# A cross-attention block on one core: where batch sums are kept, how many buffers two weights have, and when 4 MB of loads are issued

## The chip, the cores and the metric

The kernel runs on one core of a Trainium2 chip. A core has five engines that run side by side, each with its own instruction queue in program order: PE (TensorE, matrix products), DVE (VectorE), ACT (ScalarE), POOL (GpSimd) and SP (SyncE, which here only issues transfers). Sixteen DMA engines move data; SP, POOL and ACT hand them transfers through their queues. The metric is device time in microseconds (us), as the median of several executions; shorter is better. One further execution was recorded by the hardware profiler, and all lines shown come from it.

## The reference

One transformer block, all float32, with 4 batches of 512 rows, width 512, 16 heads of 32, and an MLP of inner width 2048. The mask is all ones. Cut to what matters:

```python
x = layer_norm(hidden, ln1_w, ln1_b)
q, k, v = x @ q_w + q_b, enc @ k_w + k_b, enc @ v_w + v_b      # split into 16 heads
attn = softmax(where(mask, q @ k.T / sqrt(32), lowest))
hidden = (attn @ v) @ cproj_w + cproj_b + hidden               # the batch's sum
y = layer_norm(hidden, ln2_w, ln2_b)
y = gelu(y @ fc_w + fc_b) @ proj_w + proj_b
return hidden + y
```

What matters here is `hidden` after the attention: it is read by the second layer norm, and added once more at the very end, after the MLP.

## The kernel before, in words

**Tiling.** A batch of 512 rows is four tiles of 128 rows (t = 0 to 3). The 16 heads are four groups of four (128 columns). The main loop runs over 16 steps w (batch w // 4, head group w % 4), and each step over four query tiles qt; u = 4w + qt counts them all. For each u, `scores` (L228) makes four score matrices on PE, DVE adds the mask and takes the minimum (L240), ACT takes the exponential (L244), and `turn` (L248) transposes the result in 32 x 32 blocks on DVE (L272). Two query tiles make a pair, number 2w + half. `copies` (L300) then sends the pair through 16 transfers of 136 KB (L314) on SP's queue, which put the blocks where the next product wants them: in the single buffer `pT`, or in the spare space of `gt` or `xe`. `attend` (L337) is the product with V; it is due two or four query tiles after its pair.

**What fills PE between.** For each step three projections are made ahead of it: `prep_k`, `prep_q`, `prep_v` (L191, L200, L211), from weights Wk, Wq, Wv that `load_w` (L181) loads for one head group at a time, 256 KB each. Wk has two buffers, Wq and Wv one each: Wq of step w + 1 is loaded by a call in `prep_q(w)` behind the products that read the old one (L206), and Wv likewise (L221). Then there are the output projection `cproj` (L391), the turning of layer-norm results, and the MLP of batches 0 and 1 in pieces: `fc` (L447) and `proj` (L458), 32 pieces a batch, of about 3.5 us of PE each. The MLPs of batches 2 and 3 run at the end (`last_mlps`, L509).

**The order** is written out by hand. `first[w]` and `later[w]` (L759 to L828) are lists of pieces with costs; L830 to L857 spread them over the four query tiles of the step. Every engine does its share in the order in which the calls are made, and a queue that must wait holds up all behind it. `Q[0]` is the queue for loads: POOL's until step 1, then SP's (L834). A transfer on SP also waits for the eighth one before it to have landed.

**The batch's sum.** For batch 0 the rows of x are loaded in step 3 into tiles `hid` (six buffers), get the bias of the output projection from POOL (`add_row`, L369), then `cproj`'s result from DVE (L396); the MLP later adds to the same tiles. For batches 1 and 2 the rows go to tiles `ct` (`load_ct`, L380, which also has POOL add the bias); `cproj` adds to them and stores each tile to a DRAM tensor `xa` (L398). The layer norm works in place in tiles 2 and 3, and on copies of tiles 0 and 1 loaded back from `xa` (`load_yn`, L400). When the MLP needs the sum, `load_hid` (L371) loads all four tiles back from `xa`. Batch 3 is like 1 and 2, with its sum taken to a tile of its own at the end.

**Before step 0** (L732 to L756) SP issues Wk, the encoder rows, Wv, x, Wq, the bias rows and the mask of batch 0. POOL issues Wk of step 1. The eight first MLP weights (2 MB) are POOL's, in step 0 (`load_mlp`, L436); the output projection's weights `wc` (1 MB) are SP's, in step 2; the `hid` rows of batch 0 (1 MB) SP's, in step 3.

Of the kernel before, what the change touches and what calls it, by code (L numbers as in the profile page):

```python
# [44 lines left out]
P = 128  # L45
# [29 lines left out]
def xattn_block(ctx: ExitStack, tc: tile.TileContext, x, encT, mask, q_w, k_w, v_w, c_w, fc_w, p_w, vecs, rows, out):  # L75
# [105 lines left out]
    def load_w(w, queue=None, names=("wk", "wq", "wv")):  # L181

        if w >= NW:
            return
        g = w % NG
        for n, src in (("wk", k_w), ("wq", q_w), ("wv", v_w)):
            if n in names:
                S[n, w] = (two if n == "wk" else one).tile([P, ND, P], F32, tag=n, name=f"{n}_{w}")
                (queue or Q[0]).dma_start(out=S[n, w], in_=src[:, g, :, :])
# [10 lines left out]
    def prep_q(w):  # L200
        b, g = divmod(w, NG)
        qT = kqp.tile([P, L], F32, tag="qT", name=f"qT_{w}")
        acc = acc_tile(f"accq_{w}")
        for d in range(ND):
            nc.tensor.matmul(acc, S["wq", w][:, d, :], xT[:, d, :], start=(d == 0), stop=(d == ND - 1))  # L205
        load_w(w + 1, names=("wq",))  # L206

        nc.scalar.activation(qT, acc, AF.Identity, bias=qb[:, g : g + 1], scale=-scale)  # L208
        S["qT", w] = qT

    def prep_v(w):  # L211
# [9 lines left out]
        load_w(w + 1, names=("wv",))  # L221
# [148 lines left out]

    def load_hid(b, ts_):  # L371

        for t in ts_:
            if ("hid", b, t) not in S:
                S["hid", b, t] = hids.tile([P, D], F32, tag="hid", name=f"hid_{b}_{t}")
            Q[0].dma_start(out=S["hid", b, t], in_=S["xa", b][ts(t, P), :] if b else x[b, ts(t, P), :])
        for t in ts_:
            add_row(S["hid", b, t], 1 if b else 0)

    def load_ct(b, *ts_):  # L380

        for t in ts_:
            if t == 0:
                S["xa", b] = dram.tile([L, D], F32, tag=f"xa{b}", name=f"xa{b}")
            pool, tag = (tiles, "xn") if b == B - 1 or t > 1 else (two, "ct")
            S["ct", b, t] = pool.tile([P, D], F32, tag=tag, name=f"ct_{b}_{t}")
            Q[0].dma_start(out=S["ct", b, t], in_=x[b, ts(t, P), :])
        for t in ts_:
            add_row(S["ct", b, t], 0)

    def cproj(b, t):  # L391
        h = S["ct" if b else "hid", b, t]
        acc = acc_tile(f"accc_{b}_{t}")
        for g in range(NG):
            nc.tensor.matmul(acc, S["oT", b][:, g, ts(t, P)], wc[:, g, :], start=(g == 0), stop=(g == NG - 1))  # L395
        nc.vector.tensor_tensor(h, acc, h, ALU.add)  # L396
        if b:
            (nc.sync if b == B - 1 else nc.gpsimd).dma_start(out=S["xa", b][ts(t, P), :], in_=h)  # L398

    def load_yn(b):  # L400

        S["yn", b] = [S.get(("ct", b, t)) for t in range(NT)]
        for t in range(2):
            S["yn", b][t] = tiles.tile([P, D], F32, tag="xn", name=f"xn2_{b}_{t}")
            Q[0].dma_start(out=S["yn", b][t], in_=S["xa", b][ts(t, P), :])

    def stat2(b, t):
        ln_stat((2, b), t, S["hid", b, t] if b == 0 else S["ct", b, t] if b == B - 1 else S["yn", b][t])

    def norm2(b, t):  # L410
        if b == 0 and t == 0:
            S["yn", b] = [tiles.tile([P, D], F32, tag="xn", name=f"xn2_{b}_{i}") for i in range(NT)]
        if b == B - 1 and t == 0:
            S["yn", b] = [S["ct", b, i] for i in range(NT)]
        ln_norm((2, b), t, S["yn", b][t], S["yn", b][t] if b else S["hid", b, t])

    def proj_bias(b):
        for t in range(NT):
            add_row(S["hid", b, t], 1)
# [274 lines left out]
    def A(w):  # L694
        if w >= NW:
            return []
        return do(lambda: load_w(w + 1, names=("wk",))) + [
# [48 lines left out]
    load_w(1, names=("wk",))  # L746
# [18 lines left out]
    first[0] = do(load_mlp) + do(lambda: load_w(2, names=("wk",))) + [(CHAIN, lambda: prep_v(1)), (CHAIN, lambda: prep_q(1))] + x1 + [load2, k2, q2]  # L765
    first[1] = x2[:1] + [v2, load3, k3] + x2[1:2] + [q3] + x2[2:] + [v3] + x4 + x3
    first[2] = do(lambda: Q[0].dma_start(out=wc, in_=c_w)) + [load4, q4, k4, v4] + A(5)[:2]
# [12 lines left out]
    def ct(b, *ts_):  # L780
        return do(lambda: load_ct(b, *ts_))

    def yn(b):
        return do(lambda: load_yn(b))
# [12 lines left out]
    first[3] = x1 + first[3][:2] + hid_(0, 0, 1, 2, 3) + first[3][2:]  # L797
# [6 lines left out]
    first[5] += t2 + do(lambda: proj_bias(0)) + some(5)  # L804
# [12 lines left out]
    first[10] = [load, k, q] + some(5) + [v] + yn(1)  # L817
# [42 lines left out]
    load_ct(B - 1, *range(NT))  # L860
# [10 lines left out]
    sum_wa(0)  # L871
    run(C(B - 1))
    load_hid(NORMAL, range(NT))
# [46 lines left out]
```

## Time and profile before

| | us |
|---|---|
| median of 3 runs | 839.91 (839.0 to 839.98) |
| the profiled execution's own time | 839.08 |
| its span, first to last instruction | 837.3 |
| PE busy | 813.2 (97% of the span) |
| DVE busy | 555.6 (66%) |
| ACT busy | 342.6 (41%) |
| POOL busy | 103.6 (12%) |
| mean granted PE clock | 0.990 |

The page begins with the busy time of each engine and then cuts the span into 40 slices of 20.9 us; each digit is a busy share in tenths. `PEclk` is the clock that PE was granted, in tenths. Other views are the list of waits (who waited for whom), and timelines of one engine: start, duration, engine, line, operation, tiles written and read, number of instructions, and in brackets the idle time before and what ended it. A product that the code writes as four matmul calls shows as x8; "q" in `SPq` and `POOLq` marks the issuing of a transfer, not its run. The step boundaries in this execution, by the first scores of each: step 1 at 48.8 us, 2 at 78.9, 3 at 101.8, 4 at 137.3, 5 at 178.9, 8 at 291.9, 9 at 337.4, 12 at 448.4.

### The profile page before, as it was taken

How to read it: one execution, taken by the hardware profiler on the slowest of the kernel's cores; microseconds unless marked ns; L12 is line 12 of the kernel's file. 1: busy time of each engine (PE TensorE's matmuls, PEld its weight loads, DVE VectorE, ACT ScalarE, POOL GpSimd, SP SyncE). 2: the span in 40 equal slices, each digit the busy share in tenths (PEclk: the TensorE clock that was granted, in tenths of full speed). 3: DMA queues.
4: the chain of work that ended last, by engine and by line, in shares of the span. 5: the costliest groups of instructions: out<-in, count | busy, mean ns of one | idle time of the engine just before them, and what ended most of it. 6: DMA issues, size and time to landing. Idle time of an engine off the chain costs nothing.

```text
span 837.3 us, 11995 instructions
## 1 busy us (share of the span) xinstructions
PE 813.2 (97%) x4064; PEld 473.7 (57%) x4064; DVE 555.6 (66%) x1259; ACT 342.6 (41%) x740; POOL 103.6 (12%) x122
## 2 busy tenths in 40 slices
PE   9998979799999989999999999999999999999998
PEld 6545544545444544454545445444446888888887
DVE  3597977687666666766787676787425998168511
ACT  2556554336663554346534556464301331023300
POOL 2501003102000020200010410000022003100011
PEclk9999989999999998999999999999999999999999
DMA  5658597665777766677786976885835551032001
GB/s 205 210 151 242 126 255 207 175 153 144 189 177 212 191 185 181 184 196 187 185 221 158 293 185 161 212 194 134 223 122 190 170 184 44 9 92 76 14 13 38
DMA packets 59164, 135.83 MB, mean 162 GB/s; under 512 B 12080, under 2 KB 14256, under 8 KB 58976
## 3 DMA queue, kind: packets, MB, share of 16 engines
q1 hardware_dynamic: 55920, 125.35, 55.2%
q0 software_dynamic: 2656, 8.59, 3.0%
q10 hardware_dynamic: 528, 1.14, 0.6%
q8 instruction: 32, 0.52, 0.3%
q14 instruction: 28, 0.23, 0.1%
HBM read 60.84 MB, written 7.34 MB: 81 GB/s over the span
## 4 chain that ended last, share of the span: by engine, by line
PE 89%; DVE 4%; SPq 3%; DMA 3%; issue 1%; POOL 0%; ACT 0%; DVEq 0%; ACTq 0%; POOLq 0%
PE accp L461 13%; PE accf L451 13%; PE q L555 12%; PE sc L235 7%; PE av L357 7%; PE accc L395 7%; PE accq L205 6%; PE accv L217 5%; PE acck L196 5%; SPq L314 3%; PE tp L137 2%; PE q4p L595 2%; PE q3p L595 2%; PE q5p L595 2%; PE q6p L595 2%; PE q1p L595 2%
## 5 line engine op out<-in xcount | busy, mean ns | idle before, releaser
L244 ACT ACTIVATE s<-s,mn 128x512 f32<-128x512 f32 x256 | 181.6, 710 | 157.2 <-DVE mn L240 156.9
L240 DVE CUSTOM_DVE_ANT_0 s<-sc,mb 128x512 f32<-128x512 f32 x256 | 161.3, 686 | 52.4 <-PE sc L235 52.4
L272 DVE STREAM_TRANSPOSE tb<-s 128x512 f32<-128x512 f32 x240 | 152.6, 683 | 4.2 <-ACT s L244 4.2
L451 PE MATMUL accf<-yT,fcw 128*128 128x512 f32 x256 | 115.3, 600 | 0.4 <-DVE yT L140 0.4
L461 PE MATMUL accp<-pw,gt 128*128 128x512 f32 x256 | 114.3, 598 | 0.0
L451 PEld LDWEIGHTS accf<-yT,fcw 128*128 128x128 f32 x256 | 47.0, 190 | 66.0 <-issue 60.7
L461 PEld LDWEIGHTS accp<-pw,gt 128*128 128x128 f32 x256 | 47.5, 190 | 63.2 <-issue 60.5
L235 PE MATMUL sc<-kT,qT 32*128 32x512 f32 x512 | 73.3, 642 | 1.4 <-ACT qT L208 0.8
L217 PEld LDWEIGHTS accv<-wv,xe 128*128 128x128 f32 x512 | 60.2, 196 | 15.2 <-issue 13.9
L217 PE MATMUL accv<-wv,xe 128*128 128x128 f32 x512 | 62.1, 281 | 5.4 <-DMA wv<-v_w_dram 5.4
L205 PE MATMUL accq<-xe,wq 128*128 128x512 f32 x128 | 60.9, 621 | 4.9 <-DMA wq<-q_w_dram 4.9
L555 PE MATMUL q<-ys,gt 128*128 128x256 f32 x256 | 60.2, 379 | 0.0
L196 PE MATMUL acck<-xe,wk 128*128 128x512 f32 x128 | 58.7, 601 | 0.0
L395 PE MATMUL accc<-wc,oT 128*128 128x512 f32 x128 | 56.8, 596 | 0.0
L357 PE MATMUL av<-pT,v 128*32 128x256 f32 x864 | 53.9, 391 | 0.0
L555 PEld LDWEIGHTS q<-ys,gt 128*128 128x128 f32 x256 | 48.7, 190 | 6.6
L224 POOL TENSOR_TENSOR v<-v,row 128x512 f32<-128x512 f32 x16 | 20.5, 1282 | 238.4 <-ACT v L222 238.4
L465 DVE TENSOR_TENSOR hid<-accp,hid 128x512 f32<-128x512 f32 x32 | 21.9, 684 | 40.2 <-PE accp L461 38.9
L244 ACT ACTIVATION_READ_ACCUMULATOR s<-s,mn 128x1 f32 x256 | 47.7, 186 | 0.0
L205 PEld LDWEIGHTS accq<-xe,wq 128*128 128x128 f32 x128 | 24.5, 198 | 39.1 <-issue 34.9
L555 PE MATMUL q<-yT,gt 128*128 128x256 f32 x192 | 46.4, 379 | 0.0
L244 ACT ACT_TABLE_LOAD x19 | 24.4, 1283 | 47.4 <-DVE mn L240 47.4
(122 smaller groups left out, 870.1 us busy)
## 6 DMA issues: line engine op xcount, KB each, us to landing
pT<-tb SPq DMA_DIRECT2D x400, 136.0 KB, 2.4
pw<-p_w_dram SPq DMA_DIRECT2D x32, 256.0 KB, 3.5
gt<-fc_w_dram SPq DMA_DIRECT2D x32, 256.0 KB, 2.9
gt<-tb SPq DMA_DIRECT2D x48, 136.0 KB, 3.0
fcw<-fc_w_dram SPq DMA_DIRECT2D x24, 256.0 KB, 3.1
xe<-encT_dram SPq DMA_DIRECT2D x16, 256.0 KB, 3.8
pb<-p_w_dram SPq DMA_DIRECT2D x16, 256.0 KB, 4.0
wv<-v_w_dram SPq DMA_DIRECT2D x14, 256.0 KB, 2.9
```

The costliest lines, as they stand in the source:

```text
L196: nc.tensor.matmul(acc, S["wk", w][:, d, :], eT[:, d, :], start=(d == 0), stop=(d == ND - 1))
L205: nc.tensor.matmul(acc, S["wq", w][:, d, :], xT[:, d, :], start=(d == 0), stop=(d == ND - 1))
L217: nc.tensor.matmul(acc[:, ts(t, P)], eT[:, d, ts(t, P)], S["wv", w][:, d, :], start=(d == 0), stop=(d == ND - 1),)
L235: nc.tensor.matmul(sc[:, h, :], qT[r, ts(qt, P)], kT[r, :], start=True, stop=True)
L240: nc.vector.tensor_tensor_reduce(out=s, in0=sc[:, h, :], in1=S["mb", w // NG], scale=1.0, scalar=FMAX, op0=ALU.add, op1=ALU.min, accum_out=mn,
L244: nc.scalar.activation(s, s, AF.Exp, bias=mn, scale=-1.0, accum_out=sums[:, qt, h : h + 1])
L272: nc.vector.transpose(tv[:, q, h], S["ps", w, qt][h])
L357: nc.tensor.matmul(av[ts(h, HD), : 2 * P].rearrange(shape, **kw), v[:, t, ts(h, HD)], p[t][h], start=(t == 0), stop=(t == NT - 1),)
L395: nc.tensor.matmul(acc, S["oT", b][:, g, ts(t, P)], wc[:, g, :], start=(g == 0), stop=(g == NG - 1))
L451: nc.tensor.matmul(acc, S["fcw", b, f][:, d, :], S["yT", b][:, d, :], start=(d == 0), stop=(d == ND - 1))
L461: nc.tensor.matmul(acc, gT[q % 2][:, k, ts(t, P)], S["pw", b, q * FQ + k], start=(k == 0), stop=(k == FQ - 1))
L555: nc.tensor.matmul(o, a[:, k], y[:, k], start=(k == 0), stop=(k == 1))
```

## The change

1. Wq and Wv have two buffers like Wk, and one call at the head of a step's pieces issues the three loads for step w + 1 together. The calls inside `prep_q` and `prep_v` are gone.
2. Before step 0, Wq and Wv of step 1 are issued on POOL's queue beside Wk; and the eight first MLP weights, the rows of x for batch 0's sum, and `wc` (2 + 1 + 1 MB) are issued on SP's queue behind the mask.
3. Tiles 0 and 1 of batches 1 and 2 are loaded into the `hid` buffers and stay there: they aren't stored to `xa`, not loaded back for the layer norm (which now writes to other tiles), and not loaded back for the MLP. Their MLP bias is added by POOL after the layer norm. Tiles 2 and 3 go through `xa` as before.
4. The output projection's bias is no longer added where the rows are loaded but by `c_bias`, called just before `cproj`'s pieces (batch 0: at the end of step 3's).
5. In the MLP's order, step 7 gets six pieces in place of five, so that all later pieces come one place earlier, and in step 11 one piece is moved ahead of the layer norm's turning. The last part of the loop has seven pieces left in place of eight.

In the lists `cb(b)` calls `c_bias(b)`, `h_` calls `load_h`, and `pb_(b)` calls `proj_bias(b)`, which now passes over tiles that don't stay; before, batch 0 alone called it.

```diff
-                S[n, w] = (two if n == "wk" else one).tile([P, ND, P], F32, tag=n, name=f"{n}_{w}")
+                S[n, w] = two.tile([P, ND, P], F32, tag=n, name=f"{n}_{w}")
...
     def prep_q(w):
...
-        load_w(w + 1, names=("wq",))
...
     def prep_v(w):
...
-        load_w(w + 1, names=("wv",))
...
+    def stays(b, t):
+        return b == 0 or b < B - 1 and t < 2
+    def load_h(b, *ts_):
+        if ("xa", b) not in S:
+            S["xa", b] = dram.tile([L, D], F32, tag=f"xa{b}", name=f"xa{b}")
         for t in ts_:
+            pool, tag = (hids, "hid") if stays(b, t) else (tiles, "xn")
+            S["h", b, t] = pool.tile([P, D], F32, tag=tag, name=f"h_{b}_{t}")
+            Q[0].dma_start(out=S["h", b, t], in_=x[b, ts(t, P), :])
+            if stays(b, t):
+                S["hid", b, t] = S["h", b, t]
+    def c_bias(b):
+        for t in range(NT):
+            add_row(S["h", b, t], 0)
     def cproj(b, t):
-        h = S["ct" if b else "hid", b, t]
+        h = S["h", b, t]
...
-        if b:
+        if not stays(b, t):
             (nc.sync if b == B - 1 else nc.gpsimd).dma_start(out=S["xa", b][ts(t, P), :], in_=h)
...
     def norm2(b, t):
+        h = S["h", b, t]
+        y = tiles.tile([P, D], F32, tag="xn", name=f"xn2_{b}_{t}") if stays(b, t) else h
+        S.setdefault(("yn", b), {})[t] = y
+        ln_norm((2, b), t, y, h)
...
     def A(w):
-        return do(lambda: load_w(w + 1, names=("wk",))) + [
+        return do(lambda: load_w(w + 1)) + [
...
     load_mask(0, nc.sync)
-    load_w(1, names=("wk",))
+    load_w(1)
+    Q[0] = nc.sync
+    load_mlp()
+    load_h(0, *range(NT))
+    nc.sync.dma_start(out=wc, in_=c_w)
+    Q[0] = nc.gpsimd
...
-    first[0] = do(load_mlp) + do(lambda: load_w(2, names=("wk",))) + [(CHAIN, lambda: prep_v(1)), (CHAIN, lambda: prep_q(1))] + x1 + [load2, k2, q2]
+    first[0] = do(lambda: load_w(2)) + [(CHAIN, lambda: prep_v(1)), (CHAIN, lambda: prep_q(1))] + x1 + [load2, k2, q2]
-    first[2] = do(lambda: Q[0].dma_start(out=wc, in_=c_w)) + [load4, q4, k4, v4] + A(5)[:2]
+    first[2] = [load4, q4, k4, v4] + A(5)[:2]
-    first[3] = x1 + first[3][:2] + hid_(0, 0, 1, 2, 3) + first[3][2:]
+    first[3] = x1 + first[3] + cb(0)
...
-    first[7] = [load, k, q] + some(5) + [v]
+    first[7] = [load, k, q] + some(6) + [v]
-    first[8] = ct(1, 0, 1) + [load, k] + x2[:1] + [q] + x2[1:2] + some(1) + x2[2:] + [v] + x3 + x4 + ct(1, 2, 3)
-    later[8] = C(1)
+    first[8] = h_(1, 0, 1) + [load, k] + x2[:1] + [q] + x2[1:2] + some(1) + x2[2:] + [v] + x3 + x4 + h_(1, 2, 3)
+    later[8] = cb(1) + C(1)
-    first[10] = [load, k, q] + some(5) + [v] + yn(1)
+    first[10] = [load, k, q] + some(5) + [v]
-    first[11] += norm(1, 2, 3) + some(1) + t2 + [v] + some(1)
+    first[11] += norm(1, 2, 3) + some(2) + t2 + pb_(1) + [v]
-    first[12] = ct(2, 0, 1, 2, 3) + [load, k] + some(3) + hid_(1, 0, 1)
-    later[12] = C(2)
+    first[12] = h_(2, 2, 3, 0, 1) + [load, k] + some(3)
+    later[12] = cb(2) + C(2)
-    first[14] = yn(2) + some(5) + stat(2, 0, 1) + some(2) + stat(2, 2, 3) + rs(2) + some(1)
+    first[14] = some(5) + stat(2, 0, 1) + some(2) + stat(2, 2, 3) + rs(2) + some(1)
-    first[15] = norm(2, 0, 1) + some(4) + norm(2, 2, 3) + some(4) + turns2(2)
+    first[15] = norm(2, 0, 1) + some(4) + norm(2, 2, 3) + some(4) + turns2(2) + pb_(2)
...
-    load_ct(B - 1, *range(NT))
+    load_h(B - 1, *range(NT))
...
+    c_bias(B - 1)
     run(C(B - 1))
-    load_hid(NORMAL, range(NT))
+    load_hid(NORMAL, (2, 3))
```

More of the change, by code (lines that the diff above doesn't have):

```diff
@@ L369, in add_row, with cproj @@
         nc.gpsimd.tensor_tensor(h, h, row[:, i, :], ALU.add)
+    def stays(b, t):
[3 more added lines that the diff above has]
+            S["xa", b] = dram.tile([L, D], F32, tag=f"xa{b}", name=f"xa{b}")
+        for t in ts_:
+            pool, tag = (hids, "hid") if stays(b, t) else (tiles, "xn")
[6 more added lines that the diff above has]
+            add_row(S["h", b, t], 0)
+    def cproj(b, t):
+        h = S["h", b, t]
+        acc = acc_tile(f"accc_{b}_{t}")
+        for g in range(NG):
+            nc.tensor.matmul(acc, S["oT", b][:, g, ts(t, P)], wc[:, g, :], start=(g == 0), stop=(g == NG - 1))
+        nc.vector.tensor_tensor(h, acc, h, ALU.add)
+        if not stays(b, t):
+            (nc.sync if b == B - 1 else nc.gpsimd).dma_start(out=S["xa", b][ts(t, P), :], in_=h)
     def load_hid(b, ts_):
@@ L375, in load_hid @@
                 S["hid", b, t] = hids.tile([P, D], F32, tag="hid", name=f"hid_{b}_{t}")
-            Q[0].dma_start(out=S["hid", b, t], in_=S["xa", b][ts(t, P), :] if b else x[b, ts(t, P), :])
+            Q[0].dma_start(out=S["hid", b, t], in_=S["xa", b][ts(t, P), :])
         for t in ts_:
[L378 to L389, printed above, removed]
@@ L391, in cproj @@
-    def cproj(b, t):
-        h = S["ct" if b else "hid", b, t]
[L393 to L396, printed above, removed]
-        if b:
[L398 to L405, printed above, removed]
+            add_row(S["hid", b, t], 1)
@@ L407, in stat2 @@
     def stat2(b, t):
-        ln_stat((2, b), t, S["hid", b, t] if b == 0 else S["ct", b, t] if b == B - 1 else S["yn", b][t])
+        ln_stat((2, b), t, S["h", b, t])
     def norm2(b, t):
[L411 to L415, printed above, removed]
+        h = S["h", b, t]
@@ L417, in proj_bias @@
+        y = tiles.tile([P, D], F32, tag="xn", name=f"xn2_{b}_{t}") if stays(b, t) else h
+        S.setdefault(("yn", b), {})[t] = y
+        ln_norm((2, b), t, y, h)
     def proj_bias(b):
         for t in range(NT):
-            add_row(S["hid", b, t], 1)
+            if stays(b, t):
+                add_row(S["hid", b, t], 1)
     def ln2_turn(b, d):
@@ L778, in hid_, with h_, cb, pb_ @@
         return do(lambda: load_hid(b, ts_))
[L780 to L784, printed above, removed]
+    def h_(b, *ts_):
+        return do(lambda: load_h(b, *ts_))
+    def cb(b):
+        return do(lambda: c_bias(b))
+    def pb_(b):
+        return do(lambda: proj_bias(b))
     def rs(b):
@@ L803, in xattn_block @@
     first[5] = stat(0, 0, 1) + [load, q] + stat(0, 2, 3) + rs(0) + [k] + norm(0, 0, 1, 2, 3) + [v]
-    first[5] += t2 + do(lambda: proj_bias(0)) + some(5)
+    first[5] += t2 + pb_(0) + some(5)
     load, k, q, v = A(9)
```

## The prediction

> **What bounds the kernel now.** First the page's engine row and slices, to see which engine sets the time; then PE's own waits; then the timelines of the queues at those waits.
>
> ```profile
> PE 813.2 (97%) x4064; PEld 473.7 (57%) x4064; DVE 555.6 (66%) x1259; ACT 342.6 (41%) x740; POOL 103.6 (12%) x122
> ...
> PE   9998979799999989999999999999999999999998
> ...
> PEclk9999989999999998999999999999999999999999
> ```
>
> PE is the bound: only its idle and slow stretches can be won, whatever is saved elsewhere. Slices 6, 8 and 15 (counted from 1; 104.7, 146.5 and 293 us on) hold its gaps, and the clock digit dips in 6 and 16, the latter just after the third gap. The list of waits of PE names their causes:
>
> ```profile
> PE accv L217 <- DMA wv<-v_w_dram: 5.4, 1, 5.4
> PE accq L205 <- DMA wq<-q_w_dram: 4.9, 1, 4.9
> PE tp L137 <- DVE xn L128: 4.0, 2, 3.6
> ```
>
> Three single waits. PE's timeline there (start, duration, idle before in brackets) shows that each costs more than its idle time:
>
> ```profile
> 122.63 6.16 PE L205 MATMUL accq<-xe,wq 128*128 128x512 f32 x8 [4.89 <-DMA wq<-q_w_dram]
> 128.72 1.93 PE L357 MATMUL av<-gt,v 128*32 128x256 f32 x32
> ...
> 135.42 1.93 PE L357 MATMUL av<-pT,v 128*32 128x256 f32 x32
> ...
> 151.94 5.24 PE L217 MATMUL accv<-wv,xe 128*128 128x128 f32 x32 [5.38 <-DMA wv<-v_w_dram]
> ...
> 312.01 2.60 PE L137 MATMUL tp<-ident,xn 128*128 128x128 f32 x8 [3.64 <-DVE xn L128]
> 314.55 3.64 PE L357 MATMUL av<-pT,v 128*32 128x256 f32 x32
> ```
>
> The same groups take 3.60 (accq), 3.77 (accv), 1.04 (8 tp) and 1.93 (av) elsewhere. SP's timeline says why the two weights are late, POOL's why the third wait is there:
>
> ```profile
> 103.94 0.44 SPq L189 DMA_DIRECT2D wk<-k_w_dram  x1
> 104.47 10.05 SPq L314 DMA_DIRECT2D gt<-tb  x16
> 114.57 2.03 SPq L155 DMA_DIRECT2D xn<-x_dram  x4
> 116.69 0.38 SPq L189 DMA_DIRECT2D wq<-q_w_dram  x1
> 117.17 0.38 SPq L189 DMA_DIRECT2D wv<-v_w_dram  x1
> 117.64 12.73 SPq L314 DMA_DIRECT2D pT<-tb  x16
> ```
>
> ```profile
> 307.68 1.26 POOL L369 TENSOR_TENSOR ct<-ct,row 128x512 f32<-128x512 f32 x1 [1.10 <-DMA ct<-x_dram]
> 309.04 0.19 POOL L122 TENSOR_SCALAR ve<-mv 128x4 f32<-128x4 f32 x1
> 309.31 1.03 POOL L124 TENSOR_TENSOR rs<-ve,nhalf 128x4 f32<-128x4 f32 x1
> ```
>
> Wq of step 6 stands behind 16 copies (about 0.63 us of issue each) and lands 5.8 us after its issue. Batch 3's layer norm had its statistics at 301.2 on DVE, but POOL sat in front of its reciprocal root with the bias add on `ct`, whose load SP issued only at 302.6.
>
> **The change part by part.**
>
> *Weights, the wait for Wq (step 3).* Wk, Wq, Wv of step 6 are now issued together after the pT copies that end at 103.3, ahead of the gt copies. Wq lands some 5 us later (5.1 median around there), at about 109; it is wanted at 117.7. That gives back 4.89 + (6.16 - 3.60) = 7.45. But the next wait stands close behind. PE then reaches the product for pair 6 (the pT line at 135.42) 7.45 earlier, at 127.9; and its copies, the last SP line above, end issue at 130.37 and land about 2.4 later, at 132.8. They hardly move: SP loses two weight issues ahead of them (2 x 0.48) and gets two more ahead of the gt copies. In transfers, 243 GB/s ran at 93% busy from 117 to 131 with 3.40 MB. Without Wq, Wv and `hid` in there 2.63 MB remain, 10.8 us from 117.1, but one weight more (0.26 MB, 1.1 us) comes before. So the last issue is at about 129.0 and the landing at 131.4; by issue alone, four queue groups of 1.5 + 10.05 + 2.03 + 10.05 after 103.3 and 2.4, it would be 129.3, and unchanged 132.8. I take 131.2: a new wait of 3.3 us (1.4 to 4.9). Is it followed by slow products? The rows: the waits of 3.64, 4.89 and 5.38 were, by 3.57 (1.56 + 1.71 + 0.30 in the scores), 2.56 and 1.47, at a granted clock of 0.50 to 0.53; the one of 1.60 (at 65.4) wasn't. The Trainium skill ("TensorE: Matmul & The Clock Gate", Part 1: The HAM clock gate) puts PE at half clock after at least one idle window of about 3.4 us. By that rule 3.3 costs nothing more (new wait 3.3); by the nearest row, 3.64, it costs 3.57 (6.9). The windows run free, so both can be; I take 1.5. Sum: -7.45 + 3.3 + 1.5 = **-2.6** (ends -7.4 and 0: the copies can't land later than before).
>
> *Weights, the wait for Wv (step 4).* Wv of step 7 was behind 16 gt copies (issued 148.87). Now it goes ahead of them, at about 130; wanted at 147. Its cost was 5.38 + (5.24 - 3.77) = 6.85. Late next: DVE's layer norm of batch 2, which ended at 151.3, 12.95 us after that step's first scores ended (138.35), while PE is there 3.54 + 3.53 + 1.07 + 3.77 = 11.9 after them. DVE had a backlog of 0.5 (the bias mask and sums in front) that it won't have now, so some 0.5 of wait stays. The gt copies of pair 7 are issued from about 130.3 to 141, land by 144, and are wanted at 149. **-6.4** (-6.9 to -5.0).
>
> *Bias add moved off the layer norm's way (step 8).* The adds now stand behind the reciprocal root and behind `v`'s bias on POOL. Cost of the wait: 3.64 + 1.56 + 1.71 + 0.30 = 7.2. Statistics ended at 301.2, root + 1.2, and DVE is at the norm after its scores at 303.8; one piece of the MLP ahead of it is now an add on DVE (684 ns) that PE releases at 304.6, so the norm ends about 308, where PE wants it at 308.4. What waits behind: `cproj`'s adds in step 8, from 324 on, for which four POOL adds of 1.26 are in time for tiles 0 and 1, while tiles 2 and 3 wait for the same late load as before (335.4). **-7.0** (-7.2 to -4.0).
>
> *Loads before step 0.* PE is full there but for 0.37 us; the chain is x (landing 10.1), statistics, root, norm, turning at 17.16, and Wv landed at 9.5 for a product at 9.6: no slack. The window's row:
>
> ```profile
> 5.00:10.00 5.00, 5.00 (x25) 3.04 (x24) 0.00 (x0) 0.91 (x2) 0.00 (x0) 1.00 0.98 347
> ```
>
> The last two figures are DMA share and GB/s: full. Wq and Wv of step 1 (512 KB) go on POOL's queue at about 2.2 and 2.8 us, before SP has issued x. If queues were served in SP's order they would cost 0. The Trainium skill ("DMA: Bandwidth & Descriptors", Queues, rings and completion order) says that each DMA engine goes round the queues that have work, packet by packet; then they take their share before x is done: 0.52 MB / 347 = 1.5 us. This speaks against the change, and I follow it. POOL no longer issues Wv (0.61) between root and bias add, which may pull the norm by 0.4. **+1.1** (-0.3 to +1.8). The 4 MB behind the mask need 4.2 / 347 = 12 us, from about 14 to 27, where the DMA share was 0.17 and 0.12 (15 to 25 us); without that cover they would meet the copies at 49 us. SP has 13 more issues there and is otherwise idle until 49.28: **0**.
>
> *Work with cover.* Twelve transfers of 256 KB fewer (stores 4, layer-norm loads 4, MLP loads 4): no row of PE's waits names `xa`, so **0**; they lighten SP and DMA in steps 8 to 14. In the two instruction lists ACT has six table loads more: 6 x 1.28 = 7.7 us, under ACT's 59% idle; uncovered they would cost that. The MLP order: the same products, **0** (-1 to +1). A new wait: SP's load of tile 0 of batch 2 in step 12 waits for POOL's store of batch 0's tile in the same buffer. Behind it queue MLP weights and pair 24's copies. The store was issued at 434.2 and takes 3.5; SP comes there at 459: **0**.
>
> Sum: -2.6 - 6.4 - 7.0 + 1.1 = **-14.9**. The profiled execution took 839.08 (span 837.3 and 1.8 around it), so 824.2; the median is 0.83 above it, so 839.91 - 14.9 = **825.0**.
>
> **The rivals.**
>
> *A, no wait at pair 6.* If the copies land by 127.9, step 3 gives all: 825.0 - 4.8 = **820.2**. For it: fewer bytes on a full DMA. Against: 16 issues of 0.63 from 117.1 alone end at 127.2, landing at 129.5.
>
> *B, DVE takes over.* DVE was busy 32.4 of 41.6 us in step 4, 5.4 of which PE stood still, and 13.64 of 15.9 before the first wait (86%). Moved together, its norm and transposes could come late at pair 6, batch 2's norm and batch 3's norm by 2 us each: **831**. Against: DVE was idle for 8.0 us around the first wait and 3.5 after the second.
>
> *C, slower.* The new wait of SP in step 12. Pair 24's copies need 10.05 + 2.4 and were wanted at 482.8, with about 3 us to spare; a store that held SP longer would stop PE one for one. It decides once SP is held 3 + 15 = 18 us, so the store would have to land at 477, 43 us after its issue. At 20 us held: **842**. Against: the row of 3.5 us.
>
> *D, no change.* POOL's queue or x costs as much as is won: **840**; it needs about 4 MB to get ahead of x (4.2 / 347 = 12 us, and slow products after such a wait).
>
> **How the numbers follow.** Main case 0.50 (own range 822 to 829), A 0.20, B 0.19, C 0.08, D 0.03. The predicted time is the main case's. The range goes from the sum of the good ends (-7.4 - 6.9 - 7.2 - 0.3 = -21.8: 818) to 834, the sum of the bad ends (0 - 5.0 - 4.0 + 1.8 = -7.2: 832.7) and 1 for the MLP order; it leaves out C and D. A measurement here tells about 0.2% (1.7 us) from no change. Faster 0.89, same 0.03, slower 0.08.
>
> **What would show it.** PE's waits on wq, wv and xn gone; a new wait of 1.4 to 4.9 us on pT (or SP) at about 128, with slow products if it is above 3.4; first PE turning near 18.3 in place of 17.16; no PE wait between 27 and 60 on a weight; POOL's root of batch 3 within 2 us of its statistics. Wrong would be a wait on POOL's store in step 12, a DVE release of more than 1 us at the norms of batches 2 and 3, or a start over 2 us later.

## The result and the profile after

The changed kernel takes 825.94 us (median of 4 runs, 823.71 to 827.74), beside 839.94 for the kernel before in the same sitting: a ratio of 0.9834, with a 95% interval of 0.9802 to 0.9865. Two further sittings on the chip, which come below, gave 827.76 and 825.10; all 14 executions of the changed kernel lie between 822.9 and 828.5, with their middle at 826.2. The prediction was 825.0 (818 to 834).

The profiled execution of the changed kernel took 827.74, with a span of 826.0. That is 11.3 less than the 837.3 of before, while the sum of the prediction was 14.9. The page's engine row, its PE slices and its clock slices:

```profile
PE 808.1 (98%) x4064; PEld 470.4 (57%) x4064; DVE 555.1 (67%) x1259; ACT 350.2 (42%) x746; POOL 97.3 (12%) x111
...
PE   8998997999999999999999999999999999999998
...
PEclk9999999999999999999999999999999999999999
```

PE still sets the time. The dips of slices 8 and 15 are gone, and that of slice 6 has moved into slice 7 (123.9 us on). The list of waits of PE (engine, line, what it waited for: us in all, times, longest):

```profile
PE av L355 <- DMA wk<-k_w_dram: 5.4, 1, 5.4
...
PE acck L196 <- DMA xe<-encT_dram: 1.3, 2, 0.8
PE av L355 <- DMA pT<-tb: 1.1, 1, 1.1
```

The waits on wv, wq and xn, 14 us together, are not in it any more. Three new ones are: one of 5.4 in front of a product with V, one of 1.3 at the start, one of 1.1 in front of another product with V.

To see what each is worth, take the stretches between the first scores of one query tile u and those of another; all that PE waited or ran slowly in between is in them. Both kernels do the same PE work in the stretches listed, but for one MLP piece at batch 3's norm: a `proj` piece stands where an `fc` piece stood, and in the profile a product of either takes 599 ns in the mean.

| stretch (us) | before | after | difference | the prediction's term |
|---|---|---|---|---|
| start to the first scores (u = 0) | 24.29 | 25.85 | +1.56 | +1.1 |
| u = 14 to 15: Wq of step 6 | 13.98 | 6.57 | -7.41 | -7.45 |
| u = 15 to 17: pair 6 | 14.84 | 21.77 | +6.93 | +4.8 |
| u = 17 to 18: Wv of step 7 | 14.42 | 8.19 | -6.23 | -6.4 |
| u = 33 to 35: batch 3's norm | 27.35 | 19.98 | -7.37 | -7.0 |
| u = 37 to 38: step 9 | 10.06 | 11.16 | +1.10 | 0 |
| sum | | | -11.42 | -14.9 |

The span's difference is -11.3; the piece of the MLP that the changed kernel does earlier (3.5 us) cancels between the middle and the end. So the missing 3.5 us are in pair 6 (2.1), step 9 (1.1) and the start (0.5); the other terms together came out 0.2 better.

**Pair 6.** PE's timeline after (start, duration, idle before it and its releaser in brackets), then SP's:

```profile
125.80 3.84 PE L216 MATMUL accv<-wv,xe 128*128 128x128 f32 x32
135.05 3.38 PE L355 MATMUL av<-pT,v 128*32 128x256 f32 x32 [5.42 <-DMA wk<-k_w_dram]
```

```profile
106.72 10.85 SPq L312 DMA_DIRECT2D gt<-tb  x16
117.62 2.02 SPq L155 DMA_DIRECT2D xn<-x_dram  x4
119.75 12.92 SPq L312 DMA_DIRECT2D pT<-tb  x16
132.71 0.58 SPq L189 DMA_DIRECT2D wk<-k_w_dram  x1
```

The product for pair 6, which took 1.93 where it did not wait, now waits 5.42 and takes 3.38, at a mean granted clock of 0.56. The releaser is given as Wk, but the product reads `pT` and `v` alone, and Wk's load, issued right behind the copies, takes 2.8 to land: that is at 135.5, after the product has begun. The copies into `pT` end their issue at 132.67, the last of them lands at 134.46, and the product starts at 135.05. The sixteen copies took 12.92 to issue, where an undisturbed set takes 10.05. The time in between is on SP, behind the four loads of x. Their issue (ns each) and their landing (us: shortest, median, longest), before the change:

```profile
L155 SPq DMA_DIRECT2D xn<-x_dram x4: 430/439/588, 114.6 to 116.2; - x4
DMA to landing us min/median/max: 2.9/3.2/5.1
```

and after it:

```profile
L155 SPq DMA_DIRECT2D xn<-x_dram x4: 430/439/580, 117.6 to 119.2; - x4
DMA to landing us min/median/max: 2.9/5.5/7.9
```

Six copies were issued by 123.43; the seventh, which waits for the third load of x, eight transfers before it, went out at 126.22, and that load had landed at 126.21.

**Batch 3's norm.** POOL's timeline after, and PE's:

```profile
299.59 0.19 POOL L122 TENSOR_SCALAR ve<-mv 128x4 f32<-128x4 f32 x1 [8.64 <-DVE mv L117]
299.86 1.03 POOL L124 TENSOR_TENSOR rs<-ve,nhalf 128x4 f32<-128x4 f32 x1
307.40 1.27 POOL L222 TENSOR_TENSOR v<-v,row 128x512 f32<-128x512 f32 x1 [6.51 <-ACT v L220]
308.64 2.56 POOL L367 TENSOR_TENSOR h<-h,row 128x512 f32<-128x512 f32 x2
```

```profile
306.48 1.04 PE L137 MATMUL tp<-ident,xn 128*128 128x128 f32 x8
307.45 1.94 PE L355 MATMUL av<-pT,v 128*32 128x256 f32 x32
```

The root follows the statistics at once, the bias adds (L367) come 9 us behind it, and PE turns the norm without a wait at full speed.

**Step 9.** The wait on `pT` of 1.09 goes back to POOL. DVE's timeline before and after, then SP's after:

```profile
336.72 0.69 DVE L396 TENSOR_TENSOR ct<-accc,ct 128x512 f32<-128x512 f32 x1 [5.60 <-POOL ct L369]
```

```profile
328.56 0.69 DVE L393 TENSOR_TENSOR h<-accc,h 128x512 f32<-128x512 f32 x1 [6.55 <-POOL h L367]
```

```profile
320.44 2.01 SPq L150 DMA_DIRECT2D xe<-encT_dram  x4
322.55 0.85 SPq L380 DMA_DIRECT2D h<-x_dram  x2
333.48 10.05 SPq L312 DMA_DIRECT2D pT<-tb  x16
```

The rows of tiles 2 and 3 of batch 1 are issued at 322.55, behind four encoder loads; POOL adds the bias to tile 2 at 327.26; DVE has stood 6.55 us for it (5.60 before), and in its order the transposes for a pair and the read that frees `pT` stand behind. The pair's copies start 5.2 us behind the first scores of u = 36, where they started 4.25 behind them before: about a microsecond late.

### The profile page after: what moved, and what is told of

Read it like the earlier page. It is cut to its first block, busy times and chain, and to the rows that moved or that the text cites. A ratio compares the mean times of both kernels' runs of the same rounds, so it can differ in the third digit from the quotient of the medians.

```text
span 826.0 us, 11957 instructions
## 1 busy us (share of the span) xinstructions
PE 808.1 (98%) x4064; PEld 470.4 (57%) x4064; DVE 555.1 (67%) x1259; ACT 350.2 (42%) x746; POOL 97.3 (12%) x111
## 3 DMA queue, kind: packets, MB, share of 16 engines
HBM read 58.74 MB, written 6.29 MB: 79 GB/s over the span
## 4 chain that ended last, share of the span: by engine, by line
PE 86%; DVE 5%; SPq 4%; DMA 3%; issue 1%; ACT 0%; POOL 0%; DVEq 0%; ACTq 0%
PE accf L450 13%; PE accp L460 13%; PE q L554 12%; PE sc L233 7%; PE accc L392 7%; PE av L355 7%; PE accq L205 5%; PE accv L216 4%; SPq L312 4%; PE acck L196 3%; DMA xn<-x_dram 2%; PE q4p L594 2%; PE q3p L594 2%; PE q6p L594 2%; PE q2p L594 2%; PE q1p L594 2%
## 5 line engine op out<-in xcount | busy, mean ns | idle before, releaser
L205 PE MATMUL accq<-xe,wq 128*128 128x512 f32 x128 | 58.5, 599 | 0.0
L355 PEld LDWEIGHTS av<-pT,v 128*32 128x32 f32 x864 | 26.1, 112 | 35.3 <-issue 12.3
L196 PEld LDWEIGHTS acck<-xe,wk 128*128 128x128 f32 x128 | 22.9, 190 | 34.7 <-issue 28.5
```

The costliest lines, as they stand in the source:

```text
L196: nc.tensor.matmul(acc, S["wk", w][:, d, :], eT[:, d, :], start=(d == 0), stop=(d == ND - 1))
L355: nc.tensor.matmul(av[ts(h, HD), : 2 * P].rearrange(shape, **kw), v[:, t, ts(h, HD)], p[t][h], start=(t == 0), stop=(t == NT - 1),)
```

## The experiments

Two theories stood against each other for most of the runs. The prediction's: each part of the change acts at one place, the new wait at pair 6 is set by when SP has issued its copies, and its cost grows when PE falls to half clock. The rivals: the gain at a place came from something else, or the new wait is set by the weights, by DMA traffic or by DVE. All experiments are edits of the changed kernel. All do the full computation; one of them does twelve products more that nobody uses.

What the runs gave. "First scores" is u = 0; "pair 6" is the wait in front of its product, the time that u = 15 to 17 takes over the 14.84 of before, and the part of that which is not this wait. These come from each kernel's one profiled execution, whose own time stands beside the median.

| kernel | median us (range, runs) | ratio to before, 95% | profiled us | first scores | pair 6: wait, in all, rest |
|---|---|---|---|---|---|
| changed | 825.94 (823.7 to 827.7, 4) | 0.9802 to 0.9865 | 827.74 | 25.85 | 5.42, 6.93, 1.51 |
| again | 827.76 (824.9 to 828.5, 4) | 0.9833 to 0.9878 | 827.72 | 25.66 | 4.58, 7.04, 2.46 |
| again2 | 825.10 (822.9 to 828.2, 6) | 0.9789 to 0.9845 | 826.80 | 25.62 | 3.87, 6.60, 2.73 |
| x2_early | 822.61 (821.5 to 826.8, 5) | 0.9787 to 0.9832 | 821.86 | 25.31 | 1.53, 1.60, 0.07 |
| warm6 | 824.36 (823.9 to 827.8, 4) | 0.9811 to 0.9853 | 823.86 | 25.68 | 0, 2.68, 2.68 (the added products) |
| w1_later | 825.76 (823.8 to 828.5, 5) | 0.9819 to 0.9865 | 823.81 | 24.96 | 2.24, 3.92, 1.68 |
| one_buffer | 835.56 (833.7 to 836.7, 4) | 0.9921 to 0.9962 | 833.72 | 23.88 | 0, 0, 0 |
| bias_early | 830.71 (829.0 to 831.6, 4) | 0.9865 to 0.9902 | 830.48 | 25.67 | 3.52, 3.59, 0.07 |
| roundtrip | 826.55 (824.8 to 827.7, 4) | 0.9807 to 0.9854 | 827.61 | 25.39 | 4.01, 6.77, 2.76 |
| late4mb | 828.18 (826.7 to 829.9, 4) | 0.9833 to 0.9880 | 826.86 | 25.27 | 3.53, 6.29, 2.76 |
| w1_x2 | 821.08 (819.6 to 822.7, 6) | 0.9745 to 0.9797 | 819.64 | 24.07 | 0.67, 0.73, 0.06 |
| all3 | 819.97 (818.6 to 821.0, 6) | 0.9729 to 0.9777 | 819.35 | 23.78 | 1.66, 1.72, 0.06 |

The executions of one kernel spread over 2.4 to 5.3 us, and most medians lie within one such spread of each other. Clear of all executions of the changed kernel are one_buffer and bias_early, slower, and w1_x2 and all3, faster. The rest, and the parts, are told by the stretches, each from one profiled execution.

### The changed kernel again (again, again2)

No edit: the kernel as it is, run beside the others in two sittings.

> The changed kernel once more, as the control of this group. Its four times so far lie in two pairs, 823.7 and 824.4, 827.5 and 827.7. Theory: the spread is the new wait of PE on the copies of pair 6 in step 3 and the slow products behind it (5.4 us and 1.45 us in its profile), so the median is 823.5 to 828 and the wait in this profile is between 2 and 6 us; where the time of the profiled run is near 824 its wait is about 3 us shorter than in a run near 827.7. Rival: the spread lies elsewhere, and the wait is 5.4 us again at a time near 824.

> The changed kernel itself, beside the two above: 824 to 828.5 as before, with 3 to 5 us of wait ahead of pair 6.

Measured: 827.76 and 825.10. The wait at pair 6 was 4.58 and 3.87, the product after it 3.64 both times. No execution of it near 824 came to be profiled, so it stays open whether the spread of the times is the spread of this wait. Where a stretch of another kernel is compared below, it is with the profiled execution of `again` (span 825.9).

### Two buffers for Wq and Wv taken back (one_buffer)

```diff
-                S[n, w] = two.tile([P, ND, P], F32, tag=n, name=f"{n}_{w}")
+                S[n, w] = (two if n == "wk" else one).tile([P, ND, P], F32, tag=n, name=f"{n}_{w}")
...
+        load_w(w + 1, names=("wq",))
...
+        load_w(w + 1, names=("wv",))
...
-        return do(lambda: load_w(w + 1)) + [
+        return do(lambda: load_w(w + 1, names=("wk",))) + [
...
-    load_w(1)
+    load_w(1, names=("wk",))
...
-    first[0] = do(lambda: load_w(2)) + [(CHAIN, lambda: prep_v(1)), (CHAIN, lambda: prep_q(1))] + x1 + [load2, k2, q2]
+    first[0] = do(lambda: load_w(2, names=("wk",))) + [(CHAIN, lambda: prep_v(1)), (CHAIN, lambda: prep_q(1))] + x1 + [load2, k2, q2]
```

> The changed kernel with Wq and Wv in one buffer each again (loaded inside the query and value steps, as before the change); everything else as changed. Theory: the two weights set both waits, so they come back: about 5 us on Wq in step 3 and 5 us on Wv in step 4, each followed by products at half clock; the new wait in front of the values product of pair 6 goes, and the start gains back 0.7 to 1.5 us. From the two traces the changed kernel gained 0.5 in step 3 and 6.2 in step 4 and lost 1.6 at the start, so it should be 5.1 us slower than the changed kernel: some 833. By the prediction's sizes (2.6, 6.4, -1.1) it would be 7.9 slower: some 835.5. Rival: the lighter queues of the other edits already bring the weights in time; then within 1 us of the changed kernel, some 827, with no wait on wq or wv.

Measured: 835.56. By the prediction's sizes it was to be 835.5, by those of the two traces 833; the profiled execution, the fastest of the four, took 833.72. PE's timeline:

```profile
122.32 5.69 PE L205 MATMUL accq<-xe,wq 128*128 128x512 f32 x8 [5.00 <-DMA wq<-q_w_dram]
...
134.64 1.93 PE L357 MATMUL av<-pT,v 128*32 128x256 f32 x32
...
151.72 6.37 PE L217 MATMUL accv<-wv,xe 128*128 128x128 f32 x32 [5.94 <-DMA wv<-v_w_dram]
```

Both waits are back, about as long as before the change, and the product for pair 6 between them has no wait and runs at 1.93. By stretches against `again`: 1.78 won at the start; u = 14 to 17 no different (7.06 lost on Wq, 7.04 won at pair 6); 7.94 lost on Wv. That is 6.2, and the spans differ by 6.0; the medians by 9.4 from the middle of the changed kernel's executions. So the rival, that lighter queues alone bring the weights in time, has fallen. And of the two buffers it is Wv's that pays: Wq's whole gain went into pair 6 in this comparison, because the copies for pair 6 were the next thing to be late.

### The bias adds back ahead of the root (bias_early)

```diff
-    def c_bias(b):
-        for t in range(NT):
+    def c_bias(b, ts_=range(NT)):
+        for t in ts_:
...
-    first[8] = h_(1, 0, 1) + [load, k] + x2[:1] + [q] + x2[1:2] + some(1) + x2[2:] + [v] + x3 + x4 + h_(1, 2, 3)
-    later[8] = cb(1) + C(1)
+    first[8] = h_(1, 0, 1) + do(lambda: c_bias(1, (0, 1))) + [load, k] + x2[:1] + [q] + x2[1:2] + some(1) + x2[2:] + [v] + x3 + x4 + h_(1, 2, 3)
+    later[8] = do(lambda: c_bias(1, (2, 3))) + C(1)
```

> The changed kernel with the bias adds of tiles 0 and 1 of batch 1 back right behind their loads in step 8, ahead of the reciprocal root of batch 3 on POOL. Theory (step 8): POOL waits for the two loads (issued at 300.9, landed by 306 to 308) and the root, which stood at 299.9, moves to about 308; PE waits about 3.6 us on the norm and turns at half clock after it, 7 us in all: some 834. Rival: POOL's place was harmless and PE's gain came from the MLP piece that now stands ahead of the turning; then no wait on xn and some 827.

Measured: 830.71. POOL's timeline, then PE's:

```profile
300.38 2.49 POOL L367 TENSOR_TENSOR h<-h,row 128x512 f32<-128x512 f32 x2 [12.91 <-DMA h<-x_dram]
302.95 0.19 POOL L122 TENSOR_SCALAR ve<-mv 128x4 f32<-128x4 f32 x1
303.23 1.03 POOL L124 TENSOR_TENSOR rs<-ve,nhalf 128x4 f32<-128x4 f32 x1
```

```profile
305.93 2.61 PE L137 MATMUL tp<-ident,xn 128*128 128x128 f32 x8 [2.77 <-DVE xn L128]
308.47 3.64 PE L355 MATMUL av<-pT,v 128*32 128x256 f32 x32
```

This execution runs 3.4 us ahead of `again` here (a shorter wait at pair 6, and no half clock after it), so all its times stand earlier by that. The wait on the norm is back with 2.77, shorter than the 3.6 expected, and with the slow products behind it (1.57 and 1.71) the stretch u = 33 to 34 takes 17.22 in place of 11.01: 6.2 lost, of the 7.2 that the wait cost before. The median is 4.5 above the middle of the changed kernel's executions, where some 834 was expected. POOL was held less than before the change, where the adds were done 6.3 us after SP had begun to issue the loads; here it was 5.5. The rival, that an MLP piece gave the gain, has fallen: that piece is still there.

### Transfers put back (roundtrip)

```diff
+    def back(b):
+        for t in range(2):
+            y = tiles.tile([P, D], F32, tag="xn", name=f"xn2_{b}_{t}")
+            S["y", b, t] = y
+            Q[0].dma_start(out=y, in_=S["xa", b][ts(t, P), :])
...
-        if not stays(b, t):
+        if b:
...
-    first[10] = [load, k, q] + some(5) + [v]
+    first[10] = [load, k, q] + some(5) + [v] + do(lambda: back(1))
...
-    first[14] = some(5) + stat(2, 0, 1) + some(2) + stat(2, 2, 3) + rs(2) + some(1)
+    first[14] = do(lambda: back(2)) + some(5) + stat(2, 0, 1) + some(2) + stat(2, 2, 3) + rs(2) + some(1)
```

The norm of tiles 0 and 1 reads and writes these buffers again.

> The changed kernel with eight of the twelve transfers put back: tiles 0 and 1 of batches 1 and 2 are stored to DRAM after the output projection as well, and the second layer norm reads them back from DRAM into buffers of its own. Theory: no PE wait hung on these transfers and POOL and SP have room, so 0 (-1 to +1): some 827. Rival: they delay the copies or the h loads of steps 9 to 14; then +1 to +4 with a PE wait on pT or xn between 330 and 560 us.

Measured: 826.55, within the spread of the changed kernel. Between u = 38 and the end no stretch differs by more than 0.3 us from that of `again`, and between 330 and 560 us PE has the one wait that the changed kernel has too (1.34 in step 9). The four stores and four loads cost nothing: what the title speaks of, a sum that stays on the chip, is worth nothing measurable here by itself. The other four loads saved, those for the MLP, were not put back in any run. In this profile the wait at pair 6 has its right name:

```profile
133.18 3.64 PE L355 MATMUL av<-pT,v 128*32 128x256 f32 x32 [4.01 <-DMA pT<-tb]
```

### The 4 MB back at their old places (late4mb)

```diff
-    Q[0] = nc.sync
-    load_mlp()
-    load_h(0, *range(NT))
-    nc.sync.dma_start(out=wc, in_=c_w)
-    Q[0] = nc.gpsimd
...
-    first[0] = do(lambda: load_w(2)) + [(CHAIN, lambda: prep_v(1)), (CHAIN, lambda: prep_q(1))] + x1 + [load2, k2, q2]
+    first[0] = do(load_mlp) + do(lambda: load_w(2)) + [(CHAIN, lambda: prep_v(1)), (CHAIN, lambda: prep_q(1))] + x1 + [load2, k2, q2]
...
-    first[2] = [load4, q4, k4, v4] + A(5)[:2]
+    first[2] = do(lambda: Q[0].dma_start(out=wc, in_=c_w)) + [load4, q4, k4, v4] + A(5)[:2]
...
-    first[3] = x1 + first[3] + cb(0)
+    first[3] = x1 + first[3][:2] + h_(0, 0, 1, 2, 3) + first[3][2:] + cb(0)
```

> The changed kernel with the 4 MB (MLP weights, h of batch 0, output projection's weights) back at their old places in steps 0, 2 and 3; the 512 KB of Wq and Wv of step 1 stay ahead. Theory: the late start (first scores at 25.7 in place of 24.3) comes from the 512 KB ahead of the encoder rows of step 0 and of x, so it stays within 0.4 us, and the rest gets no worse: some 827. Rival: the 4 MB fill the DMA engines from 10 to 25 us (share 1.05) and delay what step 0 still needs; then the first scores return to 24.3 to 24.8. In steps 2 and 3 the loads that return stand ahead of the x rows and copies on SP: 0 to +4 at pair 6.

Measured: 828.18, 2.0 above the middle of the changed kernel's executions, though its profiled execution is among its faster ones. The first scores are at 25.27, against 25.31 to 25.85 in the kernels that issue both the 512 KB and the 4 MB early: the 4 MB do not make the start late, or by half a microsecond at most. The median's 2.0 is within the spread. One price of the old place is seen on SP, where the four loads of h stand between the copies and the weights; on PE the next product with Wk waits for that:

```profile
130.72 2.02 SPq L380 DMA_DIRECT2D h<-x_dram  x4
132.78 0.43 SPq L189 DMA_DIRECT2D wk<-k_w_dram  x1
```

```profile
138.23 3.67 PE L196 MATMUL acck<-xe,wk 128*128 128x512 f32 x8 [1.01 <-DMA wk<-k_w_dram]
```

### Wq and Wv of step 1 issued later (w1_later)

```diff
-    load_w(1)
+    load_w(1, names=("wk",))
...
+    load_w(1, names=("wq", "wv"))
```

The second call stands behind the pieces of the first layer norm, so that POOL issues the two loads behind its root, at 15.3 us and not at 2.2.

> Only change to the changed kernel: Wq and Wv of step 1 are issued by POOL after its reciprocal root for batch 0 (about 15 us), not beside Wk at 2.2 and 2.8 us. Theory: these 512 KB share the DMA engines with the encoder rows, Wv and x at the start and cost the 1.56 us by which the first scores are later than before (25.85 against 24.29 us); then the first scores come back to about 24.3 and the time falls by 1.5 us, to 824.4. Rival: the delay comes from the 4 MB issued behind the mask, which crowd the same engines; then the first scores stay at 25.5 to 25.9 and the time stays.

Measured: 825.76, with the first scores at 24.96, 0.7 before that of `again`. A wait of 0.86 on the encoder rows remained in this execution; in the two kernels below, which have the same edit, there is none and the first scores come at 24.07 and 23.78, where one_buffer without these loads has 23.88. The last of the four loads of x lands at 14.28 in the changed kernel's profile, at 12.55 here and at 11.78 in all3 (12.11 before the change). So the 512 KB ahead of x and the encoder rows are the main cause of the late start, and cost up to 1.8. The median did not show it (824.4 was expected); it is within the spread. The row that is worth most is at pair 6:

```profile
130.99 3.55 PE L355 MATMUL av<-pT,v 128*32 128x256 f32 x32 [2.24 <-POOL v L222]
```

The releaser named, POOL's work on `v`, is for the next step's product, and in x2_early it ended at 131.12, when this product had begun at 130.63. The last copy landed at 130.42, 0.56 ahead of the start, as in the other profiles (below). After only 2.24 us of idle time PE ran the product at half speed, at a granted clock of 0.53. This is a wait at which the clock rule as weighed in the prediction would have charged nothing.

### The gap filled with products (warm6)

```diff
+            if pair == 6:
+                fill = acc_tile("fill")
+                for _ in range(12):
+                    nc.tensor.matmul(fill[:, :P], ident, ident, start=True, stop=True)
```

> Only change to the changed kernel: 12 small products of the identity with itself (about 2.6 us of PE, result not used) stand ahead of the product of pair 6, so that PE is idle for at most some 3 us there. Theory: the clock falls because PE was idle for 5.4 us; with the idle time cut the product behind it takes 1.9 us in place of 3.38, and the time falls by 0 to 1.5 us. Rival: the slow product is due to the late copies or to something else, and stays at 3.4 us; then the time is the same or up to 1 us longer.

Measured: 824.36. PE's timeline:

```profile
129.30 2.84 PE L854 MATMUL fill<-ident 128*128 128x128 f32 x24
132.08 1.93 PE L355 MATMUL av<-pT,v 128*32 128x256 f32 x32
```

PE was kept busy for the time that it would have stood, and the product ran at full speed, at a granted clock of 1.00. The stretch costs 2.68, about what the fill takes, where the changed kernel's three profiles have 6.6 to 7.0. The copies landed earlier in this execution too (the wait would have been some 2.8, not 3.9 to 5.4), so of the difference only the rest, 1.5 to 2.7, can be the clock's. One profile does not prove that the fill did it, since in bias_early the product ran at full speed after 3.52 of standing still. Of the four executions three had a mean clock of 1.0 (3 of 14 without the fill), and the fourth had 0.996 and took 827.81.

### x of batch 2 a step earlier (x2_early)

```diff
-    first[2] = [load4, q4, k4, v4] + A(5)[:2]
+    first[2] = [load4] + do(lambda: load_x(2)) + [q4, k4, v4] + A(5)[:2]
...
-    first[3] = x1 + first[3] + cb(0)
+    first[3] = first[3] + cb(0)
```

> Only change to the changed kernel: the rows of x for batch 2's layer norm (1 MB) are issued in step 2, when SP has nothing to do from 80 to 94 us, in place of just ahead of pair 6's copies in step 3. Theory: that load holds the copies up, by 2.0 us of issue and by landings of nearly 8 us for which the copies behind it wait; without it they are issued from 117.6 to 128 and land by 130.5, where PE wants them at 129.5, so the wait falls from 5.4 to about 1 us, the slow products (1.45) go, and the time falls by 3 to 6 us, to 820 to 823. Rival: the copies are bound by their own issue or by the DMA engines whatever stands ahead of them, and the wait stays at 3 us or more: 824 to 827.

Measured: 822.61. The four loads of x, 2.1 us of issue and 1 MB of traffic, no longer stand ahead of pair 6's copies. SP's timeline, then PE's:

```profile
116.97 11.31 SPq L312 DMA_DIRECT2D pT<-tb  x16
```

```profile
130.63 1.93 PE L355 MATMUL av<-pT,v 128*32 128x256 f32 x32 [1.53 <-DMA wk<-k_w_dram]
```

The copies end their issue at 128.28 and the product starts 2.35 later. That distance is the same in nearly every profile, whatever releaser is named: 2.38 in the changed kernel, 2.35 in again2, 2.36 in w1_later, 2.38 in bias_early, 2.34 in roundtrip, 2.35 in all3; only `again` (3.95) and late4mb (1.91) differ. In `again` these copies took 4.3 us to land in the median, against 2.6 in the changed kernel's profile. Counted from the landing of the last copy, `again` falls into line: there and in the eight other profiles with a wait at this place the product starts 0.56 to 0.59 behind it, and only in late4mb 0.14. So the wait at pair 6 is set by these copies, in the changed kernel by when SP can issue them, and not by Wk, Wq or POOL. Against `again`, 5.4 us were won at this place. One of the five executions still took 826.80, at a clock of 0.994.

What is left is no longer SP's loads alone. The first copy is issued at 116.97 although SP was free at 116.21, and DVE's last transpose for the pair ends at 116.91:

```profile
116.46 0.45 DVE L278 STREAM_TRANSPOSE tb<-rr 128x256 f32<-128x256 f32 x1
```

With x out of the way, it is DVE that lets these copies begin; in w1_x2 and all3 they start 0.06 behind the same transpose.

### The moves together (w1_x2, all3)

w1_x2 has the edits of w1_later and x2_early. all3 also has

```diff
-    first[8] = h_(1, 0, 1) + [load, k] + x2[:1] + [q] + x2[1:2] + some(1) + x2[2:] + [v] + x3 + x4 + h_(1, 2, 3)
+    first[8] = h_(1, 0, 1) + [load, k] + x2[:1] + [q] + x2[1:2] + some(1) + x2[2:] + [v] + x3 + h_(1, 2, 3) + x4
```

> The changed kernel with two moves: the x rows of batch 2 are loaded in step 2 in place of step 3, ahead of the copies that pair 6 waits for; and Wq and Wv of step 1 go on POOL's queue behind its first reciprocal root, not ahead of x. If the two waits are independent, 5 us from pair 6 (as the first move alone gave) and 0.8 us at the start: some 821. Rival: the moved weights fall together with the 4 MB behind the mask, so that the start gives nothing and PE only meets the same copies earlier: some 823.

> As the one with two moves, and besides the loads of tiles 2 and 3 of batch 1 go ahead of the encoder rows in step 8. If POOL's late add on tile 2 is what holds DVE, and so the sums' copies that PE waits 1.1 us for in step 9, that wait goes: some 820, 1 us below the kernel with two moves. Rival: the copies then wait for something else (ACT's k in step 9 is 1.0 us late too in the kernels without this wait on the copies), then no gain: some 821.

Measured: 821.08 and 819.97; the changed kernel beside them had 825.10. Every execution of all3 (818.6 to 821.0) is below every one of the changed kernel (822.9 to 828.2), and its ratio to the kernel before is 0.9753 (0.9729 to 0.9777). The top of PE's waits in all3, and SP's and DVE's timelines in step 9:

```profile
PE av L355 <- DMA wk<-k_w_dram: 1.7, 1, 1.7
PE tpp L256 <- ACT s L242: 1.6, 1, 1.6
```

```profile
313.23 1.02 SPq L380 DMA_DIRECT2D h<-x_dram  x2
314.30 1.85 SPq L150 DMA_DIRECT2D xe<-encT_dram  x4
322.42 10.04 SPq L312 DMA_DIRECT2D pT<-tb  x16
```

```profile
317.51 0.69 DVE L393 TENSOR_TENSOR h<-accc,h 128x512 f32<-128x512 f32 x1 [2.76 <-POOL h L367]
```

DVE stands 2.76 for POOL in place of 6.55, the copies start 1.4 us behind the first scores of u = 36 in place of 5.2, and PE's wait in step 9 is gone. In w1_x2 that wait was put down to ACT (0.96); since moving two loads on SP took it away, it was the copies there as well. By stretches against `again` all3 wins 1.88 at the start, 5.3 at pair 6 and 1.18 in step 9: 8.4, and the spans differ by 8.4. Between the two medians, 1.1 us apart with ranges that overlap, the step 9 gain is shown by the profile rather than by the times.

## Why the prediction was right, and where it was off

**The sum and its end.** 825.0 was predicted, 825.94 measured, with 825.10 and 827.76 in the other sittings. The main case (a new wait at pair 6, the rest as worked out) is what happened. In the profiled execution the sum was 3.5 us too good. That the median came within 1 us is in part luck: the profiled execution was one of the slower ones, and single executions lie up to 5.7 us apart.

**Wq (step 3).** The part that was to be won, 7.45, was 7.41. The new wait stands where it was predicted and for the reason given: the copies of pair 6 behind SP's other issues. What was mis-sized is its length: 3.3 was taken (1.4 to 4.9), and the five profiles without an edit near it (changed, again, again2, roundtrip, bias_early) show 3.5 to 5.4. The step that was off is the landing at 131.2; in the changed kernel's profile it came at 134.46, of which 1.6 is the later start. The bound "the copies can't land later than before" did not hold there either: before the change, the last one landed at 132.16. The landing was put ahead of the 132.8 of an unchanged queue because Wq, Wv and `hid` no longer shared the DMA engines; in the run gt's copies took 10.85 and pair 6's copies 12.92 to issue, where "by issue alone" counted 10.05 each. The bytes saved did not make the copies faster, because the loads of x just ahead of them needed up to 7.9 us to land (5.1 before), and a transfer on SP waits for the eighth one before it. Putting x elsewhere took 5 us of the 7 away. The slow products were taken at 1.5, as a middle between none and 3.57; they measured 1.51 in the changed kernel's profile, but 2.5 to 2.8 in again, again2 and roundtrip and 0.1 in bias_early, so the match is luck. Net, the term was -0.5 in the changed kernel's profile and not -2.6; by the profiles without an edit near it, it goes from -0.4 (again) to -3.8 (bias_early).

**Wv (step 4).** -6.4 predicted, -6.2 measured, and undoing it (one_buffer) costs 7.9. Right, down to the half microsecond that was to stay for DVE's norm of batch 2: its eight turning products take 1.65 there in place of 1.04.

**Bias add (step 8).** -7.0 predicted, -7.4 measured; undoing two of the four adds costs 6.2. Right, with its mechanism: POOL's root began 0.4 us behind the last statistics.

**Loads before step 0.** +1.1 predicted for the 512 KB, +1.56 measured, and 1.8 when taken away; 0 for the 4 MB, confirmed within 0.5. The choice between "served in SP's order" (0) and "in turns between queues" (1.5) came out for the second, although it hurts first at the encoder rows for the first products, where PE waits 1.3, which the prediction did not have. x is late too, as was said: its last rows land 2.2 us later, and in late4mb, where PE has no wait for the encoder rows, the first scores are still 1.0 later than before.

**Work with cover.** The transfers less: 0, confirmed by roundtrip for eight of the twelve. ACT's table loads: 45 in their two largest groups in place of 39, and PE's waits on ACT are the same four as before (1.6, 0.9, 0.8, 0.6). SP's wait in step 12: the h loads are issued at 451 without any hold, so rival C did not come. The step that missed 1.1 us is the one on what waits behind the moved bias adds: there the prediction said that tiles 2 and 3 wait "for the same late load as before". The wait was there before as well (5.60 of DVE), but with the norm's wait gone PE reached the next pair's product earlier, and the load had not moved as far: it became what that pair's copies waited for.

**The rivals.** A (no wait at pair 6, 820.2) did not come. The size that it set on this wait, 4.8, was there to be had: x2_early won 5.4 of the 7.0. That all3 comes out at 819.97 is no sign of A, for it still waits 1.66 at pair 6 and has 1.9 and 1.2 from two other moves. B (DVE takes over, 831) did not come: DVE's busy time is the same, and the norms of batches 2 and 3 were in time, but for the 0.6 us at batch 2's turning.

## What to carry to other kernels

When a stall is removed, look at the next instruction that waits on the same queue, and count that queue's issue time from measured rows, with what its transfers wait for, and not from an undisturbed set: here the end of the issue plus 2.35 us told the start of the product in nearly every run, whatever releaser the profile named. A load that is early enough can still cost by standing ahead of a more urgent one, so move what is not urgent into a stretch where its queue is idle, as x2_early did. Eight transfers that stood in front of no wait were worth nothing here; look for the wait before saving the traffic.

## What was not expected of the hardware

**When PE falls to half clock.** The rest in the table above (what is lost beside the wait), by length of the wait: none after 0.67, 1.53 and 1.66; 1.68 after 2.24; none after 3.52 (bias_early); 2.76 after 3.53, less the 1.01 of waiting for Wk, so 1.75; 2.76 after 4.01, 2.73 after 3.87, 2.46 after 4.58, 1.51 after 5.42. In step 8 of bias_early a wait of 2.77 was followed by 3.3 us of slow products. The granted clock over the product for pair 6 says the same: 1.00 in the runs with nothing lost, 0.53 after 2.24, 0.66 after 3.53, 0.50 to 0.56 after the longer waits; after 2.77 it was 0.50. The page "TensorE: Matmul & The Clock Gate" of the Trainium skill (Part 1: The HAM clock gate) puts half clock after at least one idle window of about 3.4 us, and calls the window free-running. The fast products after 3.52 agree with that if the wait lay across two windows, which no view shows; the slow ones after 2.24 and 2.77 contradict it, for such a wait holds no whole window of 3.4. Taken as a chance that begins between the 1.66 and the 2.24 measured, the runs fit: of the waits above, all over 2.2 us but one were followed by a lower clock, and none of the shorter ones. These are few waits, and what was lost does not grow with their length. Why an idle time shorter than the window can do it was not tested.

**How much an execution can vary by this.** Of the 14 executions of the changed kernel, the three at a mean granted clock of 1.0 took 822.9 to 824.4, and the six at 0.996 or less 826.8 to 828.5. In all3, where the wait at pair 6 is 1.66 long, five of six executions had a clock of 1.0 and the spread was 2.4. So the slower executions are, for the most part, those with more time at a lower clock (the profiled one, 827.74, had 0.998). That this time lies at pair 6 is not shown, since only one execution of each group was profiled: x2_early, with a wait of 1.53 there in its profile, spread over 5.3, and the kernel before, which has other waits, over 6.9 in one sitting.
